# Paired node-number products, shorter but fewer ties of the gathers to VectorE, and logits copied once per group

## The chip, the cores and the metric

The kernel runs on one core of a Trainium2 chip. The metric is the device time of one execution in microseconds, the median of several runs. A profile of one execution stands beside it: the page, and answers drawn from its trace. In them PE is TensorE (PEld its weight loads), DVE is VectorE, ACT is ScalarE, POOL is GpSimd and SP is SyncE.

## The reference

Two graph layers over 6250 nodes of 256 features and 106250 edges, sorted by target, 6250 of them loops. Layer 0 sends each edge's source row through a small network of the edge's type, sums by target, applies gates and three more products, and normalizes. Layer 1 is attention with four heads:

```python
h = (x @ W).reshape(n, H, F)
e = leaky_relu(a_src[src] + a_dst[dst], 0.2)
ex = exp(e - m[dst])                       # m: the largest e of a target
alpha = ex / (denom[dst] + 1e-16)          # denom: the sum of ex of a target
out = segment_sum(h[src] * alpha[..., None], dst)
x = layernorm(x + relu(layernorm(out + bias + x)))
```

## The kernel before

**Tiles, windows, groups, pairs.** The 100000 edges that are no loops lie in 782 tiles of 128. Seven tiles (`WT`) are a window, two windows a group of up to 128 target nodes. A group's sum also takes the first tile of the next group, so it has 15 tile places (`GS`). In layer 1 two groups make a pair, the last four groups stand alone.

**Prologue, to 210 us.** Edges are sorted into place, the rows of layer 0's edge network are computed for all nodes and stored (`parts0`), and the first 60 gathers of layer 0 are made.

**Layer 0, about 210 to 1163 us.** A loop makes one pass per tile. In pass n GpSimd issues the gather of tile n (`gather`, L1717: 128 rows of 256 numbers by a list of indices, into one of ten buffers `G` of seven tiles), TensorE sums tile n - 4 into its group (`sum0`, L2175: a product with a one-hot matrix that VectorE made, L1832), and all chains that are under way take one step (`Steps`). Chains are written as generators; what they yield is the number of passes they rest. `turn` (L1924 to L1942) adds the loops and transposes a group's sums, `update` (L2006 to L2137) does the gates (first multiply of the gates L2019), products and the norm of up to four groups, stores layer 1's rows (`rows1`) and writes the attention numbers of the group's nodes as bfloat16 triples to `node3` (L2137).

**Layer 1, about 1163 us to the end.** The same kind of loop. Pass t gathers tile t (L1717 again, from `rows1`), the first 21 by `gather_early`. Four passes after its gather a window's logits are copied from its rows by ScalarE (L2626) to the pair's box `e`; the first tile of the next group follows (L2618). Then `weights` starts: a transpose on TensorE (L2378), scans over the edges on VectorE (L2385 to L2396), and the exponent (L2409). `weighted` (L2424 to L2430) multiplies gathered rows by them, `sum1` (L2546) sums by target, `finish` (L2444 to L2495) normalizes and stores.

**The node numbers.** Ahead of a pair, `ahead` loads the slot numbers of its edges (0 to 127 within the group, as bfloat16 in the dram list `slots`), the same list to all 128 partitions (`dB`, L2313). 12 passes later VectorE compares them with the partition's number (`ohT`, L2338: 15 x 128 columns), and TensorE multiplies each tile's one-hot matrix by the group's `node3` (L2345: 15 products of 24 columns), which gives the attention numbers of each edge's target; VectorE adds the triples (L2355). Targets are sorted, so the first seven tiles of a group (places 0 to 6) only hold slots below 64 and places 10 to 14 only slots from 64; `MID = (7, 10)` names these bounds, and the kernel takes another path where the chip finds that they don't hold.

**The order.** Everything is issued in the order in which the loop writes it down; each engine runs its own part of that order, and waits on semaphores hold up all that stands behind on the same engine. GpSimd's gathers are tied to VectorE by hand: `Pace.passes` notes at the end of each pass the last VectorE instruction written so far, and `hold` makes the gather of pass n wait for the one noted a distance of passes sooner:

```python
def hold(self, move, n, ahead):
    n -= self.first + ahead
    if n < 0:
        return
    tc.add_manual_dep(move.ins, self.passed[n].name, ...)
```

The distance is `AHEAD0` in layer 0 and `AHEAD1` plus a term in layer 1, which falls from 42 by one in six passes and rises by one in two over the last 42 passes.

Of the kernel before, what the change touches and what calls it, by code (L numbers as in the profile page):

```python
# [42 lines left out]
P = 128  # L43
N = 6250
D = 256
# [39 lines left out]
AHEAD_G = range(AHEAD_W // 2)  # L85
LATE = 3
CR = 16 * WT
AHEAD0 = 2 * WT
AHEAD1 = WT + 1
NOROW = NP + P // 2 - 1  # L90
SORTED = "the fast path runs only where the chip has found the edges sorted"

# [1547 lines left out]
def fast(  # L1640
# [46 lines left out]
    def at(ap, offset, dims):  # L1687
        return bass.AP(tensor=ap.tensor, offset=ap.offset + offset, ap=dims)
# [58 lines left out]
    class Pace:  # L1747
# [7 lines left out]
            self.passed.append(next(i for i in reversed(traced) if i.engine == ET.DVE))  # L1755

        def hold(self, move, n, ahead):
            n -= self.first + ahead
            if n < 0:
                return  # L1760
            tc.add_manual_dep(
                move.ins,
                self.passed[n].name,
                mybir.DependencyInfo(mybir.DependencyClass.Sync, mybir.DependencyReason.DATA),
                reason="rows come no sooner than they are wanted",
            )
# [489 lines left out]
    with (  # L2256
# [45 lines left out]
        def ahead(pair, box):  # L2302

            cut = ring(ep, [P, P + 1], F32, "cut", 3)
            of = ring(ep, [P, 2 * GS, 2 * H], F32, "of", 3)
            box.update(cut=cut, of=of)
            i0, n = pair[0] % 2, len(pair)
            if i0 == 0:
                box["dB"] = ring(ep, [P, 2, GS * P], BF16, "dB", 1)
            else:  # L2310
                box["dB"] = boxes[pair[0] - 1]["dB"]
            dB = box["dB"][:, i0 : i0 + n, :]
            nc.sync.dma_start(  # L2313
                dB.rearrange("p i e -> p (i e)"),
                at(slots, pair[0] * GS * P, [[0, P], [1, n * GS * P]]),
            )
            if pair in pairs[:2]:
                for i, g in enumerate(pair):
                    nc.sync.dma_start(
                        cut[i * GS * H : (i + 1) * GS * H, :],  # L2320
                        at(cuts, tiles_in(g)[0][0] * P, [[P, GS], [0, H], [1, P + 1]]),
                    )
            else:
                o = pair[0] % 2 * GS * H
                n = ((len(pair) - 1) * GS + len(tiles_in(pair[-1])[1])) * H
                pc = ring(tps, [P, P + 1], F32, "turn", 2)
                nc.tensor.matmul(
                    pc[:n, :],
                    pick[:, pair[0] % 8 // 2, o : o + n],
                    cut_all[:, pair[0] // 8, :],  # L2330
                    start=True,
                    stop=True,
                )
                nc.scalar.copy(cut[:n, :], pc[:n, :])
            yield 12 if len(pair) > 1 else 8
            for i, g in enumerate(pair):
                ohT = ring(ep, [P, GS, P], BF16, "ohT", 2)
                nc.vector.tensor_scalar(  # L2338
                    ohT.rearrange("p j e -> p (j e)"), dB[:, i, :], iota_p, None, op0=OP.is_equal
                )  # L2340
                yield 2
                n = len(tiles_in(g)[1])
                pn = ring(ops, [P, GS, 3, 2 * H], F32, "pn", 2)
                for j in range(n):
                    nc.tensor.matmul(  # L2345
                        pn[:, j, :, :].rearrange("p c a -> p (c a)"),
                        ohT[:, j, :],
                        node3[:, g, :, :].rearrange("p c a -> p (c a)"),
                        start=True,
                        stop=True,  # L2350
                    )
                    if j == WT:
                        yield 1
                yield 1
                nc.vector.tensor_reduce(  # L2355
                    of[:, i * GS : i * GS + n, :],
                    pn[:, :n, :, :].rearrange("p j c a -> p j a c"),
                    axis=AX.X,
                    op=OP.add,
                )  # L2360
                yield 1
# [56 lines left out]
        def weighted(g, w, o, n, of, ex, top):  # L2418

            if g not in ohs:  # L2420
                ohs[g] = ring(ep, [P, (2 * WT - 2) * LOW + 3 * P], F32, "oh1", 2)
                one_hot(ohs[g], g, slot, MID[1])
            gw = ring(ep, [P, WT if n > 1 else 1, D + 2 * H], F32, f"gw{min(n, 2)}", 4)[:, :n, :]
            nc.vector.tensor_mul(  # L2424
                gw[:, :, HA:],
                top[:, o : o + n, :],
                first[:, WT * w : WT * w + n, None].to_broadcast([P, n, H]),
            )
            nc.scalar.copy(gw[:, :, D:HA], ex[:, o : o + n, :])  # L2429
            nc.vector.tensor_mul(  # L2430
                gw[:, :, :D].rearrange("p j (h f) -> p j h f", h=H),
                of[:, :n, :D].rearrange("p j (h f) -> p j h f", h=H),
                ex[:, o : o + n, :, None].to_broadcast([P, n, H, F]),
            )
            return gw

        def finish(g, ps):
# [73 lines left out]
        pair_of = {g: p for p in pairs for g in p}  # L2511
        boxes = {p[0]: {} for p in pairs}
        sums, queue, read, ohs, k3s, left, written = {}, [], set(), {}, {}, {}, []
        results = {}

        def sum1():

            while late and len(queue) < 8:
                piece = late.pop(0)
                g, w, o, n = piece[:4]  # L2520
                gw = weighted(*piece)
                queue.extend((g, WT * w + j, gw[:, j, :]) for j in range(n))
            if not queue:
                return
            g, t, gw = queue[0]
            if g not in sums and g >= 2 and g - 2 not in read:
                return
            queue.pop(0)
            if g not in sums:
                sums[g] = ring(eps, [P, D + 2 * H], F32, "fps1", 2)  # L2530
                left[g] = len(tiles_in(g)[1])
                u = everyone
                if g % 2 == 0:
                    k3s[g // 2] = ring(fp, [P, 2, 3, D], F32, "k3", 2)
                of = k3s[g // 2].rearrange("p i c f -> p i (c f)")
                if len(pair_of[g]) == 1:
                    nc.sync.dma_start(of[:, g % 2, :], kept[g // 2, :, g % 2, :])
                elif g % 2 == 0:
                    nc.sync.dma_start(of, kept[g // 2])
            begins = left[g] == len(tiles_in(g)[1])  # L2540
            left[g] -= 1
            j = t - 2 * WT * g
            to, cols = place(j, MID[1])
            ohj = ohs[g][:, cols]
            ends = left[g] == 0 or j in (WT - 1, TC - 1 - 2 * WT * g)
            nc.tensor.matmul(sums[g][to, :], ohj, gw, start=begins, stop=ends)  # L2546
            if left[g] == 0:
                run.start(finish(g, sums[g]), 1)

        def aheads():  # L2550
            for pair in pairs:
# [42 lines left out]
        while t < TC + LAG or late or queue or run.chains:  # L2594
            if EARLY <= t < TC:
                w = t // WT
                if t % WT == 0:
                    G[w] = ring(rowsp, [P, WT * HA], F32, "G", 10).rearrange(
                        "p (j f) -> p j f", f=HA
                    )  # L2600
                move = gather(G[w][:, t - WT * w, :], rows1, idx1[:, t : t + 1])
                pace.hold(move, t, AHEAD1 + max(0, 6 * WT - (t - EARLY) // 6, 3 * WT - (TC - t) // 2))
            k = t - LAG
            if 0 <= k < TC:
                if k < EARLY:
                    complete(k)
                w = k // WT
                g = w // 2
                pair = pair_of[g]
                box = boxes[pair[0]]  # L2610
                if k % (2 * WT) == 0:
                    if g == pair[0]:
                        box["e"] = ring(ep, [P, 2 * GS, H], F32, "e", 3)
                    if g:

                        old = pair_of[g - 1]
                        ob = boxes[old[0]]
                        nc.scalar.copy(  # L2618
                            ob["e"][:, old.index(g - 1) * GS + 2 * WT, :], G[w][:, 0, D:HA]
                        )  # L2620
                        if old is not pair:
                            run.start(weights(old, ob))
                if k == tiles_of(w)[0][-1]:
                    o = pair.index(g) * GS + WT * (w % 2)
                    own = len(tiles_of(w)[0])
                    nc.scalar.copy(box["e"][:, o : o + own, :], G[w][:, :own, D:HA])  # L2626
                    if w == NW - 1:
                        run.start(weights(pair, box))
            sum1()
# [67 lines left out]
```

## Time and profile before

| | |
|---|---|
| median of 9 runs | 2180.26 us (2178.31 to 2184.77) |
| the profiled execution | 2181.07 us, of which the span of its instructions 2179.3 us |
| busy over the span | PE 1586.9 us (73%), DVE 1320.1 (61%), ACT 498.8 (23%), POOL 1543.9 (71%) |
| gathers of layer 0, L1717 | 722, mean 958 ns, first 210.4, last 1130.1 us |
| gathers of layer 1, L1717 | 21 + 761, mean 956 and 961 ns, 1131.3 to 2126.6 us |
| weighted rows on VectorE, L2430 | 167, 248.9 us |
| slot comparisons on VectorE, L2338 | 56 of 128x1920, 42.1 us |
| node-number products, L2345 | 837, 41.0 us on PE |
| logit copies on ScalarE, L2626 | 112, mean 212 ns; idle 190.2 us before them, 149.8 of it for gathers |
| DMA over the span | 346.12 MB, 159 GB/s |

A row of the page's groups names the line, the engine, the operation, what is written and read with shapes and the count; behind the bar come busy time and the mean of one, then the engine's idle time just before, and what ended most of it. "issue" is time in which the engine waited for nothing that the profile shows. A row of the timeline gives start and length in us, and in brackets the idle time before it. Idle time of an engine that is not the bottleneck costs nothing, and a busy share hides the short gaps between instructions.

### The profile page before, as it was taken

The numbers are of one execution on the slowest core, as the hardware profiler recorded it, in microseconds if no ns is written. First come the engines' busy times: TensorE is split into PE (matmuls) and PEld (weight loads), VectorE is DVE, ScalarE is ACT, GpSimd is POOL, SyncE is SP. The second block draws the span as 40 slices with busy tenths as digits, with TensorE's granted clock in tenths as the row PEclk, the third lists the DMA queues.
The fourth block names the chain that finished last, engine by engine and source line by source line (L and its number), as shares of the span: only waits on it lengthen the run. The fifth ranks groups of instructions, "written<-read, shape, count | busy, mean of one in ns | idle before, by whom it ended". The sixth has DMA issues, their size and how long they took to land.

```text
span 2179.3 us, 23269 instructions
## 1 busy us (share of the span) xinstructions
PE 1586.9 (73%) x6390; PEld 850.3 (39%) x6390; DVE 1320.1 (61%) x3622; ACT 498.8 (23%) x1538; POOL 1543.9 (71%) x1610
## 2 busy tenths in 40 slices
PE   8988998788888888888986656465565555555564
PEld 5656543333433333333554333233232333333332
DVE  8854354434243433434443788888887777878786
ACT  3333132122211222122341121221211211121112
POOL 2466677777777777777777777777777777777770
PEclk9999999999899998999997777777776767677776
DMA  5355645445554555445555555555555555555551
GB/s 158 114 173 173 187 148 184 146 139 172 167 153 136 164 167 168 139 147 173 184 156 174 167 175 156 174 167 157 179 163 160 163 160 166 157 171 151 172 153 37
DMA packets 146105, 346.12 MB, mean 159 GB/s; under 512 B 36154, under 2 KB 66720, under 8 KB 145965
## 3 DMA queue, kind: packets, MB, share of 16 engines
q0 software_dynamic: 76048, 207.99, 34.0%
q1 hardware_dynamic: 67741, 133.51, 17.5%
q10 hardware_dynamic: 2176, 3.05, 0.4%
q8 instruction: 52, 0.85, 0.2%
q14 instruction: 88, 0.72, 0.1%
HBM read 291.90 MB, written 52.52 MB: 158 GB/s over the span
## 4 chain that ended last, share of the span: by engine, by line
PE 31%; DVE 21%; DMA 17%; issue 11%; POOL 8%; ACT 4%; DVEq 0%; POOLq 0%; ACTq 0%
PE fps L2175 11%; DMA G<-parts,fidx 9%; POOL G L1717 8%; DMA G<-rows,fidx 7%; PE fpg L2006 6%; DVE gw L2430 5%; PE fps L2546 4%; DVE oh L1832 3%; PE fpg L2092 2%; PE fps L2288 1%; PE fpm L1571 1%; DVE fst L2476 1%; PE fpg L2054 1%; ACT fy L2484 1%; DVE ohT L2338 1%
## 5 line engine op out<-in xcount | busy, mean ns | idle before, releaser
L1717 POOL DMA_INDIRECT G<-rows,fidx x761 | 731.1, 961 | 233.3 <-issue 132.9
L1717 POOL DMA_INDIRECT G<-parts,fidx x722 | 692.0, 958 | 230.7 <-issue 156.3
L2546 PE MATMUL fps<-gw,oh 128*64 128x264 f32 (+1 forms) x1674 | 469.5, 471 | 187.7 <-DVE gw L2430 187.7
L2175 PE MATMUL fps<-G,oh 128*64 128x257 f32 (+1 forms) x1674 | 498.2, 417 | 116.2 <-DMA G<-parts,fidx 99.0
L2546 PEld LDWEIGHTS fps<-gw,oh 128*64 128x64 f32 (+1 forms) x1674 | 241.4, 177 | 335.1 <-DVE gw L2430 202.2
L2175 PEld LDWEIGHTS fps<-G,oh 128*64 128x64 f32 (+1 forms) x1674 | 210.0, 156 | 378.4 <-DMA G<-parts,fidx 175.0
L2430 DVE TENSOR_TENSOR gw<-G,bank 128x1792 f32<-128x1792 f32 (+1 forms) x167 | 248.9, 1491 | 57.3 <-ACT gw L2429 56.0
L2006 PE MATMUL fpg<-faT,fWihT 128*128 128x512 f32 (+2 forms) x432 | 172.8, 525 | 0.2 <-DVE faT L1942 0.2
L1832 DVE TENSOR_TENSOR oh<-bank,fslot 128x448 f32<-128x448 f32 (+2 forms) x318 | 156.5, 547 | 8.9 <-ACT bank L2409 6.1
L1924 DVE TENSOR_SCALAR kind<-fps 128x1 f32<-128x1 f32 x112 | 12.4, 152 | 207.9 <-PE fps L2175 207.9
L1571 PE MATMUL fpm<-fWrT,fhT 128*128 128x256 f32 x392 | 94.9, 393 | 13.6 <-DVE fms L1579 13.3
L2126 DVE COPY nd<-hr 128x4 f32<-128x4 f32 x53 | 9.9, 188 | 152.3 <-ACT hr L2098 152.3
L2006 PEld LDWEIGHTS fpg<-faT,fWihT 128*128 128x128 f32 x432 | 73.2, 196 | 68.4 <-issue 56.5
L1557 PE MATMUL fph<-fxc,fWrT 128*128 128x512 f32 (+1 forms) x208 | 89.9, 582 | 5.1 <-DMA fWrT<-in_WrT_dram 4.6
L1605 POOL DMA_INDIRECT G<-parts,fidx x60 | 62.0, 1033 | 42.4 <-DVE fms L1579 19.0
L2345 PE MATMUL pn<-node,ohT 128*128 128x24 bf16 x837 | 41.0, 180 | 68.2 <-DVE ohT L2338 61.6
L1571 PEld LDWEIGHTS fpm<-fWrT,fhT 128*128 128x128 f32 x392 | 75.1, 196 | 33.2 <-DVE fms L1579 12.6
L2478 ACT ACTIVATE frs<-fmv,eps_c 128x1 f32<-128x1 f32 x112 | 32.9, 294 | 237.0 <-DVE gw L2424 153.6
L2484 ACT ACTIVATE fy<-fy,frs 128x256 f32<-128x256 f32 x112 | 66.9, 597 | 87.3 <-DVE frs L2481 87.0
L2378 PE MATMUL turn<-fident,e 128*120 128x128 f32 (+2 forms) x30 | 12.0, 399 | 96.2 <-ACT e L2618 96.2
L2345 PEld LDWEIGHTS <-ohT 128*128 128x128 bf16 x837 | 34.2, 103 | 109.5 <-DVE ohT L2338 76.0
L2092 PE MATMUL fpg<-Wx,fyT 128*128 128x264 f32 x224 | 72.5, 451 | 3.0 <-ACT fyT L2083 3.0
(348 smaller groups left out, 1967.9 us busy)
## 6 DMA issues: line engine op xcount, KB each, us to landing
dB<-slots SPq DMA_DIRECT2D x26, 960.0 KB
kept<-keep SPq DMA_DIRECT2D x26, 768.0 KB
k<-kept SPq DMA_DIRECT2D x26, 768.0 KB
loop<-parts SPq DMA_DIRECT2D x55, 256.0 KB
parts<-fms SPq DMA_DIRECT2D x49, 256.0 KB
G<-parts,fidx POOLq DMA_INDIRECT x782
G<-rows,fidx POOLq DMA_INDIRECT x761
out_dram<-fy SPq DMA_DIRECT2D x56, 128.0 KB
```

The source lines that it names most:

```text
L1557: nc.tensor.matmul(ph[:, :cols], WrT_s[:, r, k, m * P : (m + 1) * P], xc[:, k, :cols], start=(k == 0), stop=(k == 1),)
L1571: made = nc.tensor.matmul(pm[:, r, :], hT[:, r, k, j * P : (j + 1) * P], WrT_s[:, r, k, :], start=(k == 0), stop=(k == 1),)
L1605: nc.gpsimd.indirect_dma_start(out=of[:, n % WT, :D], out_offset=None, in_=parts0[: 2 * P * block, :], in_offset=bass.IndirectOffsetOnAxis ...
L1717: return nc.gpsimd.indirect_dma_start(out=to_tile, out_offset=None, in_=table, in_offset=bass.IndirectOffsetOnAxis(ap=idx, axis=0),)
L1832: nc.vector.tensor_tensor(to[:, o : o + len(js) * n].rearrange("p (j s) -> p j s", s=n), iota_s[:, None, cols].to_broadcast([P, len(js), n ...
L2006: nc.tensor.matmul(pg[:, :cols], WihT_s[:, k, c * P : (c + 1) * P], aT[:, k, :cols], start=(k == 0), stop=(k == 1),)
L2092: nc.tensor.matmul(ph[u, :], hs[i][:, k, u], Wx[:, k, :], start=(k == 0), stop=(k == 1))
L2175: nc.tensor.matmul(sums[g][to, :], ohj, got[t], start=begins, stop=ends)
L2345: nc.tensor.matmul(pn[:, j, :, :].rearrange("p c a -> p (c a)"), ohT[:, j, :], node3[:, g, :, :].rearrange("p c a -> p (c a)"), start=True ...
L2430: nc.vector.tensor_mul(gw[:, :, :D].rearrange("p j (h f) -> p j h f", h=H), of[:, :n, :D].rearrange("p j (h f) -> p j h f", h=H), ex[:, o ...
L2484: nc.scalar.activation(y, y, AF.Identity, bias=m, scale=r)
L2546: nc.tensor.matmul(sums[g][to, :], ohj, gw, start=begins, stop=ends)
```

## The change

Four edits. **Ties:** `AHEAD0` goes from 14 to 6 and `AHEAD1` from 8 to 4, and only gathers whose number divides by four are tied. **Products:** `dB` and `ohT` have 10 tile places in place of 15. The lower 64 partitions hold the slots of places 0 to 9; the upper 64 hold those of 10 to 14 in the first five places and their own 7 to 9; the rest of the upper half keeps the -1 of a memset. One product of the first five places serves two tiles, j and j + 10, against `node2`, whose lower rows have the node numbers in the first 24 columns and whose upper rows have them in the last 24; ScalarE fills its two blocks by two copies a group, of four buffers in turn. The list is loaded by three transfers. **Logits:** both windows of a group are copied when its second is there, the second first. **Weighted rows:** the multiply at L2430 no longer waits for the gathers of its rows, since the weights come from logits copied out of the same rows.

```diff
-AHEAD0 = 2 * WT
-AHEAD1 = WT + 1
+AHEAD0 = WT - 1
+AHEAD1 = WT - 3
+EVERY = 4
...
         def hold(self, move, n, ahead):
+            if n % EVERY:
+                return
...
-                box["dB"] = ring(ep, [P, 2, GS * P], BF16, "dB", 1)
+                box["dB"] = ring(ep, [P, 2, MID[1] * P], BF16, "dB", 1)
...
-            nc.sync.dma_start(
-                dB.rearrange("p i e -> p (i e)"),
-                at(slots, pair[0] * GS * P, [[0, P], [1, n * GS * P]]),
-            )
+            for ps, c0, j0, jn in (
+                (low_s, 0, 0, MID[1]),
+                (high_s, 0, MID[1], GS - MID[1]),
+                (high_s, MID[0], MID[0], MID[1] - MID[0]),
+            ):
+                nc.sync.dma_start(
+                    dB[ps, :, c0 * P : (c0 + jn) * P],
+                    at(slots, (pair[0] * GS + j0) * P, [[0, LOW], [GS * P, n], [1, jn * P]]),
+                )
...
             for i, g in enumerate(pair):
-                ohT = ring(ep, [P, GS, P], BF16, "ohT", 2)
+                halves = node2[g % 4]
+                for h, ps in enumerate((low_s, high_s)):
+                    nc.scalar.copy(
+                        halves[ps, h, :], node3[ps, g, :, :].rearrange("p c a -> p (c a)")
+                    )
+                ohT = ring(ep, [P, MID[1], P], BF16, "ohT", 2)
...
-                for j in range(n):
-                    nc.tensor.matmul(
-                        pn[:, j, :, :].rearrange("p c a -> p (c a)"),
-                        ohT[:, j, :],
-                        node3[:, g, :, :].rearrange("p c a -> p (c a)"),
-                        start=True,
-                        stop=True,
-                    )
-                    if j == WT:
+                po = pn.rearrange("p j c a -> p j (c a)")
+                for j in range(MID[1]):
+                    if j < GS - MID[1]:
+                        to, of_n = po[:, j : MID[1] + j + 1 : MID[1], :], halves
+                    elif j < MID[0]:
+                        to, of_n = po[:, j, :], halves[:, 0, :]
+                    else:
+                        to, of_n = po[:, j, :], node3[:, g, :, :].rearrange("p c a -> p (c a)")
+                    nc.tensor.matmul(to, ohT[:, j, :], of_n, start=True, stop=True)
+                    if j == MID[1] // 2:
                         yield 1
...
-            nc.vector.tensor_mul(
+            made = nc.vector.tensor_mul(
                 gw[:, :, :D].rearrange("p j (h f) -> p j h f", h=H),
...
+            for move in brought.get(w, [])[:n]:
+                tc.declare_no_dep(
+                    made.ins, move.ins, reason="the weights come from logits of these rows"
+                )
...
+        node2 = [ep.tile([P, 2, 6 * H], BF16, name=f"node2_{i}") for i in range(4)]
+        for halves in node2:
+            nc.vector.memset(halves, 0.0)
+        nc.vector.memset(ring(ep, [P, 2, MID[1] * P], BF16, "dB", 1), -1.0)
...
                 move = gather(G[w][:, t - WT * w, :], rows1, idx1[:, t : t + 1])
+                brought.setdefault(w, []).append(move)
...
-                if k == tiles_of(w)[0][-1]:
-                    o = pair.index(g) * GS + WT * (w % 2)
-                    own = len(tiles_of(w)[0])
-                    nc.scalar.copy(box["e"][:, o : o + own, :], G[w][:, :own, D:HA])
+                if k == tiles_of(w)[0][-1] and (w % 2 or w == NW - 1):
+                    for v in (w, w - 1) if w % 2 else (w,):
+                        o = pair.index(g) * GS + WT * (v % 2)
+                        own = len(tiles_of(v)[0])
+                        nc.scalar.copy(box["e"][:, o : o + own, :], G[v][:, :own, D:HA])
```

More of the change, by code (lines that the diff above doesn't have):

```diff
@@ L2513, in fast @@
         sums, queue, read, ohs, k3s, left, written = {}, [], set(), {}, {}, {}, []
-        results = {}
+        results, brought = {}, {}
         def sum1():
```

## The prediction

> **What bounds the kernel now.** I read the page first (costliest groups, slices), then the time by stages, the waits of GpSimd, and last the timeline of the places that these point to.
>
> ```profile
> L1717 POOL DMA_INDIRECT G<-rows,fidx x761 | 731.1, 961 | 233.3 <-issue 132.9
> L1717 POOL DMA_INDIRECT G<-parts,fidx x722 | 692.0, 958 | 230.7 <-issue 156.3
> ```
>
> ```profile
> 400.00:600.00 200.00, 170.82 (x528) 75.11 (x528) 74.24 (x260) 42.33 (x106) 151.78 (x159) 0.91 0.52 158
> ...
> 1500.00:1700.00 200.00, 113.19 (x579) 64.96 (x576) 162.77 (x399) 40.14 (x167) 151.84 (x159) 0.73 0.55 164
> ```
>
> The stages list PE, PEld, DVE, ACT and POOL, busy time and (count). TensorE leads in layer 0 and VectorE in layer 1, yet GpSimd issues 159 gathers in 200 us in both, one in 1.258 us. Its waits say that little holds it up:
>
> ```profile
> POOL G L1717 <- issue: 293.3, 963, 0.3
> ```
>
> 963 gaps, none over 0.3 us. A gather costs 0.95 + 0.30 = 1.25 us, so 76% busy is a full engine; starts of neighbouring gathers lie 1.25 us apart (median) whether the gather carries one, two or three waits. From 210 to 2127 us the kernel is a train of 722 + 21 + 761 = 1504 gathers, 1880 us of 1917. What moves the end is a stall of the train, a stretched gather, or the 53 us behind it.
>
> **Shorter ties, layer 0.** With a distance of 14 passes no tie bound here: the VectorE instruction waited for had ended 1.7 us or more before its gather. With 6 they bind at the start, where TensorE works off the sums gathered ahead and VectorE waits for it. Gathers are numbered from 60 (210.45 us), and number 96 starts at 262.04. After the change it waits for the last VectorE instruction of pass 90, by the built kernel's order the first multiply at L2019:
>
> ```profile
> 262.04 0.95 POOL L1717 DMA_INDIRECT G<-parts,fidx  x1 [0.30 <-issue]
> ```
>
> ```profile
> 269.06 0.68 DVE L2019 TENSOR_TENSOR fgg<-fgg,fgi 128x512 f32<-128x512 f32 x1
> ```
>
> It ends at 269.74. The one tie that did bind before (below) let its gather start 0.27 us after the end, so number 96 starts at 270.0, 8.0 us late. Numbers 84, 88 and 92 are late by 0.2, 2.1 and 6.1 us in the same way, which is contained in the 8.0; 104 needs 276.60 and would start at 280 anyway. All later gathers queue behind. TensorE does not notice at once:
>
> ```profile
> 250.00:270.00 20.00, 20.00 (x77) 10.50 (x76) 8.36 (x22) 3.34 (x4) 15.13 (x17) 1.00 0.56 159
> ```
>
> ```profile
> 336.95 0.65 PE L2175 MATMUL fps<-G,oh 128*64 128x257 f32 x2 [0.58 <-DMA G<-parts,fidx]
> ```
>
> It is full, and waits for a gather for the first time at 336.95. But from there to 1108 it waits for gathers again and again (99 us in all), and the train has no slack to catch up in. So a delay passes to the end of layer 0 whole, and on into layer 1, which starts from it: **+8.0 us**. Bounds: 0, if something later absorbs it, and 8.0 plus the 1.3 us of the next tie that comes close (gather at 313.5), if VectorE moves with the train.
>
> **Shorter ties, layer 1.** VectorE starts this layer behind. Measured from a gather's start to the end of its pass's last VectorE instruction it is 38 us behind at 1163, 22 at 1200, 10 at 1411, 4.5 at 1482 (medians over 28 passes, with swings of some 5 us), and from 1590 to 2050 never over 3.1. The distance falls by one pass in six gathers until about 1480, then is 8 before and 4 after. Before, it bound once:
>
> ```profile
> 1487.92 0.95 POOL L1717 DMA_INDIRECT G<-rows,fidx  x1 [0.30 <-issue]
> 1490.58 0.94 POOL L1717 DMA_INDIRECT G<-rows,fidx  x1 [1.71 <-DVE frs L2481]
> ```
>
> 2.66 instead of 1.25 us: 1.4 lost. With 4 passes less, the gather at 1485.42 waits for that same L2481 (end 1490.31, plus 0.27): 5.2 us. Against it stands that VectorE is faster by then: one-hot comparisons (L2338) take 0.715 us for 1920 columns; 1280 take between two thirds of that and no less, I take 0.22 us saved. 18 groups pass from 1163 to 1485, 18 x 0.22 = 4.0. Loss 1.2 against 1.4 before: **-0.2**. Bounds -1.4 (no tie binds) and +3.8 (VectorE gains nothing). Later, the smallest slack of a tied gather is 3.2 us, so the steady part is untouched.
>
> Fewer ties by themselves (waits on VectorE at gathers 878 to 358 in the built order) bring nothing: the 1.25 us do not depend on the number of waits.
>
> **The comparison beside the train.** The one stretched gather that repeats in layer 1 lies beside L2338:
>
> ```profile
> 1606.43 0.95 POOL L1717 DMA_INDIRECT G<-rows,fidx  x1 [0.30 <-issue]
> 1607.68 1.24 POOL L1717 DMA_INDIRECT G<-rows,fidx  x1 [0.31 <-DMA G<-rows,fidx]
> ```
>
> ```profile
> 1607.39 0.71 DVE L2338 TENSOR_SCALAR ohT<-dB,fiota_p 128x1920 bf16<-128x1920 bf16 x1
> ```
>
> Over all 56 the gathers beside L2338 exceed 0.947 us by 6.6 us together. A third less comparison takes a third of it: **-2.2 us**, bounds 0 and -6.6.
> The Trainium skill (SBUF — State Buffer, Who interferes with whom) says that such an instruction and GpSimd share a port pair as an exclusive lock, and that the later one fully blocks. By that the gather would lose the 0.42 us that L2338 still had to run, the trace shows 0.29; if every L2338 blocked for all its 0.715 us, 40 us would be lost now and 13 won, and the whole sum would be near -6. I go by the rows.
>
> **Products.** 837 products and loads become 560, 280 of them twice as wide. TensorE does eight in 0.39 us and only 2.0 us of VectorE's waits (reduction at L2355) are for them: 0, cover gone 2.0 won. The added ScalarE copies of node numbers, 112 of 0.208 us (row of L2137), are 23 us on an engine busy 23%, issued two passes (2.5 us) ahead of the products: 0; without that cover 0.4 us a group, 23 us over layer 1 if TensorE and then VectorE waited each time. Five memsets at the start of layer 1 (the widest 2560 columns; L1787 wrote 672 in 0.62, so 2.4) fall where VectorE sits idle 6.8 us until 1168.78 for its first list (L2274): 0, and 3 if that list came at once.
>
> **The slot lists.** 30 transfers of up to 960 KB become 90 of 64 partitions, 61% of the bytes. SyncE takes 0.32 us for an issue (L2313), 19 us more, and between issues it is idle for 10 us and more (1602.66 to 1624.96). Queued behind are the loads of kept rows and the output; VectorE never waited for a list (idle before L2338: 0.0), and a list is asked for 12 passes, 15 us, ahead: 0; bounds -1 and, if all three were late by an issue each, 26 x 0.64 = 17.
> The Trainium skill (DMA: Bandwidth & Descriptors, Rules for kernel authors) speaks against this edit: transfers to disjoint partition halves serialize, one of 128 partitions is to be used. With its fit of 2.0 us plus bytes over 436 GB/s, three in a row would take some 7.4 us for a pair, one 4.3 (estimates from that page); 3 us more under a cover of 15 leave the sum as it is.
>
> **Logits.** The 112 copies of 0.212 us stay; both of a group now stand behind its last gather, so ScalarE no longer stops in mid-group, and the transpose comes one copy later: 0.2 us once per pair, in layer 1's steady part inside the train's slack of 3.2 us: 0; bounds -1 and +1 at the end. The 493 waits for gathers dropped at the weighted rows (L2430) are hidden too: of 57.3 us idle before them 56.0 are ScalarE's copy, so 1.3 at most.
>
> **Behind the last gather** (2126.6 to 2179.3) VectorE and TensorE work alone, and VectorE is already 3.5 to 4.7 us behind from 2086. Five comparisons fall there: 5 x 0.22 = **-1.1**, bounds +1 and -2.
>
> **Sum.** +8.0 - 0.2 - 2.2 - 1.1 = +4.5 us. The profiled execution (2181.07 us, span 2179.3) becomes 2185.6; it lies 0.8 over the median of 2180.26, so I predict 2184.8 us.
>
> **Rivals.** (1) *The delay in layer 0 is absorbed.* TensorE is full until 336 us and again near 1000 to 1135 (122 of 130 us), and if it, not the train, sets the end of layer 0, the 8.0 costs nothing: 2180.3 - 0.2 - 2.2 - 1.1 = 2176.8, no change. With the whole 6.6 of stretched gathers won it is 2172.4, faster; the point from which it decides is 3.1 us won at the stretched gathers with layer 0 at zero. For it: 20.00 of 20 us. Against it: the waits for gathers after 336, up to 1108. 0.2 for both, 0.08 of it past the point.
> (2) *Layer 1's ties bind in full*, because VectorE's 0.22 us are lost in waits for ScalarE (idle before L2430): +3.8 for -0.2, 2188.8. Against it: VectorE is 83% busy there. 0.2.
> (3) *The comparisons hold the train for their full length*: a third of 56 x 0.715 us is 13.3 us won for 2.2, 2173.7, faster; it decides from 11.1 us won on. Against it: all stretched gathers of layer 1 together exceed by 10.4 us. 0.05.
> (4) *Three list transfers or the added copies come late* and the products with them: 17 us, 2201.8. For it: nothing but the number of issues. 0.05.
> My forecast has the remaining 0.5, from 2181 to 2188.
>
> **Numbers.** A measurement of this kernel tells 0.2% (4.4 us) from no change: faster is below 2175.9, slower above 2184.6. Faster: 0.08 of (1), 0.05 of (3) and 0.01 of the forecast: 0.14. Slower: 0.19 of (2), 0.05 of (4), and 0.27 of the forecast's 0.5, whose middle lies just above the bound: 0.51. Same: the rest, 0.35. The range reaches from (1) at 2176 to (2) with the second tie of layer 0 (1.3): 2190.
>
> **What would show it.** Right: GpSimd with one wait of some 7 to 8 us for VectorE near 262 us, gathers 1.25 us apart whatever they wait for, layer 1's first gather some 8 us later than 1163.5, no wait or one of 1 to 3 us near 1490, L2338's comparison at 0.5 us and its stretched gather at 0.2 over. Wrong: no long wait in layer 0; or layer 1 starting at 1163 in spite of it; or waits of GpSimd spread over the steady part.

## The result, and the profile after

The changed kernel takes 2192.49 us (median of 10 runs, 2189.47 to 2199.04); the kernel before, run beside it, 2181.63 (32 runs). The ratio is 1.0053, 95% interval 1.0045 to 1.0061: slower by 11 us, where 4.5 were forecast and 2190 was the upper end of the range. The profiled execution took 2190.16 us, its span is 2188.3, 9.0 more than the span before.

The page's rows of GpSimd's gathers, then a row of GpSimd's waits (us in total, times, longest):

```profile
L1718 POOL DMA_INDIRECT G<-rows,fidx x761 | 734.4, 965 | 232.7 <-issue 187.9
L1718 POOL DMA_INDIRECT G<-parts,fidx x722 | 691.6, 958 | 239.3 <-issue 178.5
```

```profile
POOL G L1718 <- issue: 370.0, 1204, 3.7
```

The longest gap put down to "issue" was 0.3 us, now it is 3.7; layer 1's gathers take 965 ns on average instead of 961, which over 761 of them is 3.3 us; layer 0's have kept their 958. So there are two places to look at: a stall in layer 0 and a stretch in layer 1. The steady middle of both layers (us; then busy time and count of PE, PEld, DVE, ACT, POOL; the granted clock of TensorE as a share of full speed, the DMA share, GB/s) is what it was, 159 to 160 gathers in 200 us. The traces have the clock at full or at half speed only, so 0.70 is a mean:

```profile
400.00:600.00 200.00, 162.73 (x531) 70.95 (x530) 74.81 (x264) 42.22 (x105) 151.57 (x160) 0.97 0.52 159
1500.00:1700.00 200.00, 108.77 (x483) 61.65 (x483) 155.37 (x394) 42.63 (x190) 151.87 (x159) 0.70 0.56 153
```

The timeline of GpSimd at the head of layer 0, rows of late gathers (0.30 is the usual gap):

```profile
249.10 0.94 POOL L1718 DMA_INDIRECT G<-parts,fidx  x1 [0.76 <-DVE faT L1945]
...
257.49 0.95 POOL L1718 DMA_INDIRECT G<-parts,fidx  x1 [3.70 <-issue]
...
265.00 0.95 POOL L1718 DMA_INDIRECT G<-parts,fidx  x1 [2.80 <-DVE faT L1945]
...
271.63 0.95 POOL L1718 DMA_INDIRECT G<-parts,fidx  x1 [1.93 <-DVE fgg L2022]
```

These are four tied gathers, four apart. Each idle time less 0.30 is the stall: 0.46 + 3.40 + 2.50 + 1.63 = 8.0 us. "issue" at 257.49 is the same wait with its releaser not found. The gather that was at 262.04 is at 271.63.

In layer 1 VectorE and GpSimd, side by side:

```profile
1734.78 0.42 DVE L2508 SCALAR_TENSOR_TENSOR fy<-fy,k 128x256 f32<-128x256 f32 x1
1735.12 0.54 DVE L2351 TENSOR_SCALAR ohT<-dB,fiota_p 128x1280 bf16<-128x1280 bf16 x1
1735.23 1.25 POOL L1718 DMA_INDIRECT G<-rows,fidx  x1 [0.30 <-DVE fy L2508]
```

The comparison is shorter as forecast (0.54 us for 0.71), and the gather that starts beside it still takes 1.25 us, 0.30 more than its neighbours. It is not the only such instruction. Line 2508 (L2490 before) runs into gathers where no comparison follows, too:

```profile
1714.70 0.42 DVE L2508 SCALAR_TENSOR_TENSOR fy<-fy,k 128x256 f32<-128x256 f32 x1
...
1714.88 1.07 POOL L1718 DMA_INDIRECT G<-rows,fidx  x1 [0.30 <-issue]
```

In the trace of before 5 gathers of layer 1 start beside it in this way and lose 0.6 us together, in that of the changed kernel 20, which lose 2.4.

The trace cut at the first and last gather of each layer gives the whole account. All times are us, and the runs below the first two rows are told of in the next section:

| kernel | first gather | layer 0's train | between | layer 1's train | end | span |
|---|---|---|---|---|---|---|
| before | 210.45 | 919.64 | 33.37 | 963.13 | 52.70 | 2179.29 |
| changed | 211.62 | 927.69 | 33.30 | 965.77 | 49.89 | 2188.27 |
| changed, again | 210.44 | 927.78 | 33.01 | 965.04 | 49.53 | 2185.80 |
| all ties back | 213.26 | 921.58 | 33.73 | 966.06 | 50.37 | 2185.00 |
| layer 0's ties back | 212.01 | 920.64 | 33.34 | 966.94 | 49.29 | 2182.22 |
| layer 0's distance back | 212.44 | 921.10 | 33.68 | 966.66 | 49.93 | 2183.81 |
| changed, beside that | 212.70 | 933.82 | 31.93 | 967.99 | 49.89 | 2196.33 |
| all ties back, comparison later | 211.58 | 922.93 | 33.11 | 958.79 | 50.12 | 2176.53 |

Between the first two rows: +1.2 ahead of the trains, +8.05 in layer 0, -0.1 between, +2.6 in layer 1, -2.8 at the end, together +9.0. The 1.2 lie in the prologue, which the change does not touch, and the second profile of the changed kernel has them not.

### The profile page after: what moved, and what is told of

Its sections match the earlier page's. It is cut to its first block, busy times and chain, and to the rows that moved or that the text cites. A ratio compares the mean times of both kernels' runs of the same rounds, so it can differ in the third digit from the quotient of the medians.

```text
span 2188.3 us, 21961 instructions
## 1 busy us (share of the span) xinstructions
PE 1574.4 (72%) x6113; PEld 839.3 (38%) x6113; DVE 1310.7 (60%) x3627; ACT 512.5 (23%) x1650; POOL 1547.0 (71%) x1610
## 4 chain that ended last, share of the span: by engine, by line
PE 29%; DVE 28%; DMA 14%; issue 9%; POOL 9%; ACT 5%; SPq 0%; ACTq 0%; DVEq 0%; POOLq 0%
PE fps L2178 9%; DMA G<-parts,fidx 9%; POOL G L1718 9%; DVE gw L2444 8%; PE fpg L2009 6%; PE fps L2564 5%; DVE oh L1835 4%; DMA G<-rows,fidx 3%; DVE fst L2494 1%; PE fpg L2095 1%; DVE ohT L2351 1%; PE fpm L1572 1%; PE fps L2291 1%; ACT fy L2502 1%; DVE fy L2479 1%
## 5 line engine op out<-in xcount | busy, mean ns | idle before, releaser
L2178 PE MATMUL fps<-G,oh 128*64 128x257 f32 (+1 forms) x1674 | 493.2, 410 | 133.2 <-DMA G<-parts,fidx 116.2
L2365 PE MATMUL pn<-node,ohT 128*128 128x24 bf16 (+1 forms) x560 | 35.6, 192 | 69.6 <-DVE ohT L2351 65.9
L2365 PEld LDWEIGHTS <-ohT 128*128 128x128 bf16 x560 | 28.5, 107 | 111.2 <-DVE ohT L2351 77.1
```

The source lines that it names most:

```text
L2178: nc.tensor.matmul(sums[g][to, :], ohj, got[t], start=begins, stop=ends)
L2365: nc.tensor.matmul(to, ohT[:, j, :], of_n, start=True, stop=True)
```

## The experiments

**The ties and the products apart, first sitting** (a sitting is a set of runs made together on one chip). Four kernels. The first puts layer 0's ties back:

```diff
-AHEAD0 = WT - 1
+AHEAD0 = 2 * WT
...
-            if n % EVERY:
+            if not self.first and n % EVERY:
```

> Theory A (the changed kernel's extra time is 8.0 us of stalls of the gather train in layer 0, and some 3 us in layer 1 that are not its ties): with layer 0 tied as before, layer 0 from its first to its last gather takes 919.6 us again instead of 927.7, and the time is 8.0 us below the changed kernel, 2 to 3 us above the kernel before. Rival B (the delay of layer 0 would have been absorbed, and something else costs the time): within 3 us of the changed kernel. Rival C (the products and lists cost what is left): as A in layer 0, so this run alone does not tell C from A.

The second puts all ties back (also `AHEAD1 = WT + 1`, and no `EVERY`):

> All ties as before; products, logits and the dropped wait as in the changed kernel. Theory A: layer 1's ties cost less than 1 us, so this is within 1.5 us of the run with layer 0's ties back; against the kernel before 1 to 3 us slower, with some 9 us of stretched gathers beside the slot comparison where the kernel before has 6.6. The prediction's own terms (2.2 us won beside the comparison, 1.1 won at the end): 3.3 us faster than before. Rival D (layer 1's ties cost the 3.8 us of the prediction's bound): 3 us or more below the run with layer 0's ties back.

The third is the kernel before with the new ties and nothing else:

> The kernel before with the ties alone. Theory A: 8.0 us in layer 0, and in layer 1 the 3.8 us that the prediction put on the ties if VectorE gains nothing (no shorter comparison here to make up for them): 11.8 us slower than before. If layer 1's ties do not bind even so: 8.0 less the 1.4 us of the one bound tie, 6.6 us slower. Rival B: within 2 us of before.

The fourth is the kernel before with the paired products and their lists and nothing else:

> The kernel before with the paired products and three list transfers alone. Prediction's terms: 3.3 us faster (2.2 beside the comparison, 1.1 at the end). Theory A (what a comparison costs the train goes by where it falls in a gather, not by its length): between 1 us faster and 3 us slower, with a comparison of 0.55 us instead of 0.72. Rival C (lists and copies come late): VectorE or TensorE waits for dB or for node copies, 3 us slower or more.

None of these theories was about the regime that these four ran in. There the kernel before took 2738.01 us (26 runs), and TensorE was granted a clock of 0.76 on average instead of 0.84. The first three ratios in the order above: 0.9923 (0.9894 to 0.9952), 0.9974 (0.9948 to 1.0), 0.9905 (0.9873 to 0.9937); products alone 0.9973 (0.9952 to 0.9994). The page of the kernel with layer 0's ties back has this chain and these slices of the clock:

```profile
PE 33%; DVE 26%; another core or an unknown queue 22%; issue 11%; ACT 4%; DMA 2%; POOL 1%; ACTq 0%; SPq 0%; DVEq 0%; POOLq 0%
...
PEclk9977988788877878879866676676766767676766
```

GpSimd is 1% of the chain there. The "unknown queue" is stretches in which TensorE begins next to nothing while VectorE and ScalarE stand still, such as the second row here, from the windows of the same kernel:

```profile
640.00:656.00 16.00, 13.09 (x55) 6.45 (x54) 8.78 (x26) 2.46 (x6) 12.04 (x14) 1.00 0.39 117
656.00:673.00 17.00, 0.34 (x2) 0.10 (x2) 0.00 (x0) 0.00 (x0) 10.03 (x11) 0.61 0.31 92
```

TensorE is busy for 0.34 us of these 17, while GpSimd goes on with 11 gathers until they too wait for VectorE. The clock was at half for 1299 us of this execution, for 701 us of that of the kernel before at 2181. But the standing still is nearly all of the longer time: this same kernel ran later at a clock of 0.84 (below), with a span of 2182.2 us instead of 2700.5, 518 less. Stretches of over 4 us in which TensorE, VectorE and ScalarE all stand still make 475 us here (55 of them, up to 16.9), and 4.8 us there (one). What they wait for the trace does not show. With the train no longer the bound, what is won or lost at the train says nothing on the forecast, and the new ties even help, 0.9905 on their own. Why they do was not settled.

**The changed kernel again.**

> The changed kernel itself, unaltered. Where the granted clock is 0.84 to 0.85 and the kernel before takes some 2181 us, every theory expects the 2192 us already seen. Where the granted clock is 0.76 and the kernel before takes some 2738 us, the theory that a full train of gathers pays for every stall expects it slower there too, by about the same 11 us; the theory that TensorE, held to half its clock for half the time, is the bound there, and that the train has slack, expects the sum of what its parts did there: layer 1's ties -16 us, layer 0's -7 us, the rest -5 us, so some 2710 us, a ratio of 0.990.

Measured at a clock of 0.84: 2190.69 us, the kernel before 2181.46, ratio 1.0048 (1.0031 to 1.0064). The result repeats, and the layer-0 train repeats to 0.1 us.

**Four once more, and the clock at 0.76 again.** The kernel before took 2765.86 us in this sitting. Layer 0's ties back:

> The changed kernel with layer 0's ties put back to a distance of 14 and onto every gather; layer 1 keeps the new ties. Measured before this run: 2181 us for the kernel before, 2191 to 2192 for the changed one. Theory 1 (four stalls of GpSimd at the head of layer 0, 8.0 us, come straight off the end): 2183 to 2184. Rival (layer 0's stalls are taken up by slack between the layers, and the loss sits in layer 1): 2190 to 2192.

0.9894 (0.9867 to 0.9921). All ties back:

> The changed kernel with all ties as before: only the paired products, their lists, the logits' copies and the dropped wait are left of the change. Theory 1 (what layer 1 lost comes with the paired products, whose shorter comparisons now fall on a gather each): the layer-1 train still 2.5 us longer than before, the end 2 to 3 us shorter, so 2181 to 2184, and within 1 us of the run with layer 1's ties kept. Rival (layer 1's shorter and fewer ties cost it): 3 us or more below that run, at 2178 to 2181.

2747.25 us, 0.9934 (0.9913 to 0.9954). Products alone:

> The kernel before with the paired products and their lists alone; ties, logits and waits as before. If the products bring the stretch of layer 1's gathers, the layer-1 train is 2 to 3 us longer here as well and the time is that of the run with all ties back, within 1 us. If the logits' copies or the dropped wait bring it, the train is as before (963 us) and the time 2 to 3 us lower.

2746.14 us, 0.9939 (0.9913 to 0.9965). All ties back, with the comparison made twice instead of 56 times:

```diff
+                ohT = ohT_made.get(g % 2)
+                if ohT is None:
+                    ohT = ohT_made[g % 2] = ring(ep, [P, MID[1], P], BF16, "ohT", 2)
...
```

> All ties back, and the comparison of line 2351 made for two groups only and reused for the other 54, so its output is not the reference's. Theory 1 (a gather that starts beside a comparison is lengthened by it, and the train is the bound): the excess of layer 1's gathers over 0.946 us falls by the 9 us that stood beside comparisons, to some 4 or 5 us, and the time by 8 to 10 us below the run with all ties back. Rival (another VectorE instruction moves into its place and stretches the gather as much): less than 3 us below. Second rival (VectorE's 31 us of comparisons delay the sums and so the end): more than 12 us below.

2729.85 us, 0.9878 (0.9854 to 0.9903): 17 us below the run with all ties back, where theory 1 had 8 to 10 and the second rival more than 12. The excess of layer 1's gathers over 0.946 us is 1.3 us in its trace and 6.3 in that with all ties back, so shorter gathers make 5 us of the 17 at most. The forecasts in us fail here as in the first sitting. Two things carry over: with and without the logits' copies and the dropped wait the kernel takes the same time in both sittings (2747.25 and 2746.14; 2733.04 and 2730.36), so these edits do nothing that can be measured there; and the regime belongs to the sitting and not to the chip, since the chip of these four ran the next experiment at 2187 us for the kernel before.

**All ties back, at a clock of 0.84.**

> All ties as before; the paired products, their lists, the logits' copies and the dropped wait stay. Where the granted clock is 0.84 and the kernel before takes 2181 us: theory 1 (ties cost 8.0 us in layer 0 and nothing in layer 1; the paired products' comparisons lengthen layer 1's gathers by some 3 us and the end gives 2 to 3 back) 2181 to 2184, a layer-0 train of 920 us, a layer-1 train of 965 to 966 us; rival (layer 1's shorter and fewer ties lengthen its train) 2178 to 2181 and a layer-1 train of 963 us or less. Where the clock is 0.76: 0.993 to 0.997 of the kernel before, as in the two runs there.

2185.94 us beside 2187.17, ratio 0.9995 (0.9984 to 1.0006). So what the change makes slower is in the ties; the rest of it together does nothing that the interval shows. Its trains say how: 966.06 us in layer 1, as long as with the new ties. Layer 1's 2.6 us are not from the ties, which the rival said. They come with the rest, and the end gives them back. Products, logits and the dropped wait were not taken apart at this clock, so which of them moves layer 1 and the end is not shown.

**The comparison, 0.2 us later.** In the trace with all ties back I set the start of each comparison against the start of the last gather before it, and the two gathers around it against the usual 0.946 us. The loss is a matter of when the comparison starts. From 0.95 to 1.15 us the next gather is longer by what the comparison still has to run beside it, less 0.12 to 0.14 us, in 38 cases of 38; from 0.5 to 0.94 next to nothing; from 0.08 to 0.25 at most 0.05; the two at 0.41 and 0.46 lengthen the gather that is running, by 0.13 and 0.17. In the kernel before, 17 comparisons start at 1.17 to 1.22 us, that is 0.03 to 0.08 us ahead of the next gather, and lengthen nothing. The changed kernel has none there and 24 at 1.05 to 1.15, the dearest place. A rule of the Trainium skill (SBUF — State Buffer, Who interferes with whom) is an exclusive lock in which the later one waits in full; the gather that starts second does lose here, but 0.13 us less than the overlap, and from 1.17 us on nothing, although the comparison still starts first. To test it, one instruction that does nothing useful goes ahead of each comparison:

```diff
+                nc.vector.tensor_add(lull, iota_f, iota_f)
                 ohT = ring(ep, [P, MID[1], P], BF16, "ohT", 2)
...
+        lull = ep.tile([P, P], F32, name="lull")
```

> All ties as before, products and logits as changed, and one more VectorE instruction (a sum of two 128x128 f32 tiles, some 0.19 us) ahead of each of the 56 comparisons of line 2351, so that each starts 0.19 us later. In the profile with all ties back, 23 comparisons start 1.07 to 1.13 us after the start of the last gather and lengthen the next one by 0.23 to 0.29 us, 15 start at 0.95 to 1.01 us and lengthen it by 0.12 to 0.18 us, and those that start at 0.02 to 0.23 us lengthen nothing. Theory P (where in the gather's 1.25 us the comparison falls decides, not how long it is): the 23 move to 0.01 to 0.07 us of the next gather and cost nothing, the 15 to 1.14 to 1.20 us and cost 0.3 us each or nothing, so the excess of layer 1's gathers beside comparisons falls from 8.5 us to between 1 and 6 us and the time by 3 to 8 us, although VectorE has 10 us more to do. Rival (each comparison beside the train costs by its length alone, whenever it comes): the excess stays at 8 to 9 us and the time within 1 us. Second rival (VectorE's extra 10 us reach the end): 2 to 10 us slower.

2177.42 us beside 2183.75: 0.9971 (0.9962 to 0.998). More work, and faster than both kernels; against all ties back (0.9995) it is 5.2 us by the ratios, which were measured in two sittings. The same place in the two timelines, first with all ties back, then with the instruction added:

```profile
1802.12 0.43 DVE L2506 SCALAR_TENSOR_TENSOR fy<-fy,k 128x256 f32<-128x256 f32 x1
1802.46 0.55 DVE L2349 TENSOR_SCALAR ohT<-dB,fiota_p 128x1280 bf16<-128x1280 bf16 x1
...
1802.61 1.22 POOL L1718 DMA_INDIRECT G<-rows,fidx  x1 [0.30 <-DVE fy L2506]
```

```profile
1797.17 0.42 DVE L2507 SCALAR_TENSOR_TENSOR fy<-fy,k 128x256 f32<-128x256 f32 x1
1797.51 0.28 DVE L2348 TENSOR_TENSOR lull<-fiota 128x128 f32<-128x128 f32 x1
1797.71 0.55 DVE L2350 TENSOR_SCALAR ohT<-dB,fiota_p 128x1280 bf16<-128x1280 bf16 x1
...
1797.67 0.95 POOL L1718 DMA_INDIRECT G<-rows,fidx  x1 [0.30 <-DVE fy L2507]
```

The comparison is as long as it was. It starts 0.15 us ahead of a gather above, 0.04 us behind one below, and the gather takes 0.95 us for 1.22. The starts say the same: the next gather follows 1.52 us later above (1804.13) and 1.25 us later below (1798.92). Over layer 1:

```profile
L1718 POOL DMA_INDIRECT G<-rows,fidx x761 | 735.3, 966 | 232.0 <-issue 126.5 <-DVE gw L2436 14.9 <-DVE sm L2462 11.3
```

```profile
L1718 POOL DMA_INDIRECT G<-rows,fidx x761 | 727.3, 956 | 232.8 <-issue 111.2 <-DVE gw L2437 15.2 <-DVE frs L2498 11.8
```

8.0 us less of gather time, and a train of 958.79 for 966.06. By the place of the comparison (us after the last gather's start; number of comparisons, and what the gathers around them lost in us):

| | 0 to 0.35 | to 0.48 | to 0.94 | to 1.05 | to 1.165 | later | sum |
|---|---|---|---|---|---|---|---|
| before | 8: 0.3 | 1: 0.3 | 17: 1.9 | 13: 4.2 | 0 | 17: 0 | 6.7 |
| changed | 4: 0 | 2: 0.3 | 12: 0.1 | 14: 2.0 | 24: 6.7 | 0 | 9.1 |
| all ties back | 4: 0.1 | 2: 0.3 | 12: 0 | 15: 2.2 | 23: 6.0 | 0 | 8.6 |
| comparison later | 19: 0.3 | 1: 0.1 | 19: 0.1 | 4: 0.7 | 7: 2.2 | 6: 0 | 3.4 |

Theory P holds on the place, within its 1 to 6 us of excess and 3 to 8 us of time; both rivals fall. How sharp the place is shows in the last row: the 6 that start at 1.16 us cost 0.33 us each, the 6 from 1.18 us nothing. Its words "not how long it is" go too far: at 0.95 to 1.05 us a comparison of 0.71 us costs 0.32 us (13 of them, before), one of 0.55 us 0.14 (14, changed). At a given start the shorter one does cost less; the starts moved.

The comparison is 5.2 of the 8.0 us. Line 2508 follows the same rule (L2506 with all ties back, L2507 here): it takes 0.42 us, and 21 of them start 1.04 to 1.07 us after a gather's start with all ties back and cost 2.2 us together. In the run with the instruction added 3 do, for 0.3 us, and 14 start at 0.43 to 0.45 and cost nothing, as 18 do before at 0.44 to 0.46. So the delay moved more than the comparison, and helped at both.

**Layer 0's ties back, at a clock of 0.84.**

> The changed kernel with layer 0's ties put back to a distance of 14 and onto every gather; layer 1 keeps the new ties. The changed kernel took 1.0048 and 1.0053 of the kernel before, and with all ties back 0.9995. Where the granted clock is 0.84: theory 1 (the four stalls at the head of layer 0 are the whole cost of the ties, 8.0 us or 0.0037) a layer-0 train of 920 to 922 us, a layer-1 train of 965 to 966 us, and 0.999 to 1.001; rival (the ties cost in layer 1 too, the 3 to 4 us by which 1.0053 over 0.9995 exceeds 8.0 us) 1.001 to 1.003.

2184.7 us beside 2184.91: 0.9997 (0.9988 to 1.0006). Layer 0's ties are the whole of the loss; layer 1's new ties cost nothing that the times show, 0.9997 against 0.9995 with them back. In its profile two of them do bind, for 2.3 us together, where with all ties back none does, and its layer-1 train is 966.94 us, 0.9 longer and just over the 965 to 966 of theory 1.

**Distance or number of ties, on one chip.** By those ratios layer 0's ties cost 11 to 12 us, and the stalls in the profile are 8.0. One kernel has the changed line `AHEAD0 = 2 * WT` and nothing else undone, the other is the changed kernel.

> The changed kernel with layer 0's distance alone put back to 14 passes; still only every fourth gather is tied, in both layers. Theory 1 (the distance of 6 makes GpSimd wait for VectorE at the head of layer 0; how many gathers are tied brings and costs nothing): a layer-0 train of 918 to 922 us and 8 to 12 us less than the changed kernel beside it, 0.999 to 1.001 of the kernel before. Rival (part of the 10 to 12 us by which the changed kernel's time stood above the run with layer 0's ties back, more than the 8.0 us of stalls in its profile, comes from tying only every fourth gather): 2 to 4 us above 1.000.

> The changed kernel, unaltered, on the same chip as the run with layer 0's distance back, so that the cost of that distance is read from times of one sitting and from two profiles of it. If the stalls at the head of layer 0 are all: the layer-0 train 8 us longer than in that run and the medians 8 us apart. If the distance costs elsewhere too: the medians 10 to 12 us apart, and the trains or the stretch before the first gather show where.

With the distance back: 2184.76 us, 1.0011 (1.0002 to 1.002). The changed kernel beside it: 2193.71 us, 1.0046 (1.0033 to 1.006). The distance of 6 costs 8.95 us by the medians, between the two forecasts of 8 and of 10 to 12. The changed kernel's profile, of the longest of its five executions (2198.12 us), has the four stalls of 8.0 us and others later, the largest of 2.87 us:

```profile
1030.25 0.69 DVE L2022 TENSOR_TENSOR fgg<-fgg,fgi 128x512 f32<-128x512 f32 x1 [5.39 <-ACT fgg L2017]
...
1031.21 0.94 POOL L1718 DMA_INDIRECT G<-parts,fidx  x1 [3.17 <-DVE fgg L2022]
```

The tied gather starts 0.27 us after L2022 ends, as at the head of the layer. The stretch of time just before, in this execution and in that of the kernel with the distance back:

```profile
1005.00:1020.00 15.00, 12.97 (x35) 6.34 (x34) 5.05 (x29) 4.21 (x11) 11.35 (x13) 0.76 0.75 229
```

```profile
1005.00:1020.00 15.00, 15.00 (x42) 5.63 (x40) 3.81 (x10) 6.22 (x11) 11.34 (x13) 1.00 0.59 189
```

The clock was 0.76 in one and 1.00 in the other. That a slower TensorE made VectorE late enough for the tie to bind is what these rows suggest; it is one execution, and was not forced. What they show is that the distance of 6 leaves room for such stalls in the middle of the layer, of which the other two profiles of the changed kernel have some 0.1 us at most. Those two are of executions 2.3 and 3.0 us under their medians, this one 4.4 over. The 11 to 12 us against 8 can thus be in part stalls that come in some executions; the rest is within the ratios' own uncertainty of some 2 us. Whether the number of ties counts for anything stays open. 1.0011 lies just outside theory 1's range and at the lower end of the rival's 2 to 4 us; the layer-0 train, 921.10 us, is theory 1's. With every gather of layer 0 tied it was 0.9997, on another chip, and the two intervals overlap.

## Why the prediction failed, step by step

**Layer 0's ties, +8.0: right in the profile, short in some executions.** Same gathers, same instructions of VectorE, 8.05 us in the profile, and 8.0 us at layer 1's first gather once the prologue's 1.2 are taken off: the 33 us between the layers did not shrink. Nothing absorbed it (rival 1). I had named one wait of 7 to 8 us near 262; it was spread over four waits, which the same paragraph had counted as contained in the 8.0. The upper bound of 9.3 was too low: one execution lost 12.7 (933.82 against 921.10), 1.6 of it in longer gathers. I had looked for ties that nearly bind in one trace alone.

**Layer 1's ties, -0.2: within the bounds.** The one wait before was 1.4 us, the one after is 1.15 - 0.30 = 0.85:

```profile
1496.60 0.95 POOL L1718 DMA_INDIRECT G<-rows,fidx  x1 [1.15 <-DVE frs L2499]
```

This moves from execution to execution: with the new ties in layer 1 the waits are 0.8 us in the second profile of the changed kernel, 2.3 and 2.2 in the two runs with layer 0 put back, 3.4 in the changed kernel beside the latter. Against the 1.4 of before that is -0.6 to +2.0 us. Rival 2's 3.8 us did not come, and undoing the ties there moved nothing in the times. The 0.22 us that each comparison was to save were 0.17 (0.546 for 0.715, medians).

**The comparison beside the train, -2.2: this step failed.** The loss beside it was to fall by 2.2 us; it rose from 6.7 to 9.1 us, and with other stretched gathers layer 1's excess went from 11.2 to 14.5. The words "a third less comparison takes a third of it" treat the loss as a share of the comparison's length. The dear part is the overlap with a gather that has yet to start, so it is set by the comparison's length and above all by where it starts in a cycle of 1.25 us; the step had no term for the start. The change moved 24 of them to the dearest place and took 17 from the one where they cost nothing. The sum also had the other stretched gathers at no change; beside L2508 they went from 0.6 to 2.4 us, for the same reason. Why the starts moved was not taken apart; it was not the ties, since they lie there with all ties back as well. The trace of before had it all: 17 comparisons at 1.17 to 1.22 us with no stretched gather were in it, and I looked only at the sum. My bounds, 0 and -6.6, excluded a loss for no reason that I had given. Rival 3, a lock for the comparison's full length, had the same fault from the other side.

**Behind the last gather, -1.1:** -2.8. The bound was -2. At the measured 0.17 us the five comparisons are 0.9; what the other 1.9 are was not looked into. All runs with products, logits and the dropped wait at this clock have an end of 49.3 to 50.4 us, so it repeats.

**Products, lists, logits, dropped wait, 0: right in sum.** With all ties back the ratio is 0.9995, which is layer 1's loss and the end's gain together. An issue of a list took 0.60 us (median) where 0.32 was reckoned, and the lists have 60% of the bytes, not 61; of the 90 transfers VectorE waited for one, for 5.7 us at the start of layer 1, ahead of a layer that begins with a backlog. (The Trainium skill's rule in DMA: Bandwidth & Descriptors, Rules for kernel authors, spoke against three transfers for one; going against it cost nothing that shows here. The same page gives the fit that the prediction used for transfers issued by GpSimd; these are SyncE's, and no run here has their duration.)

**The sum.** 8.05 - 0.1 + 2.6 - 2.8 + 1.2 = 9.0 in the profile against +4.5: 4.5 us more. Layer 1's train is 5.0 us off (+2.6 for -2.4), which is the comparison's step and its like: 2.4 more beside the comparison, 1.9 beside L2508, about 1 less at other gathers and 0.6 less at the tie. The prologue's variation adds 1.2, and the end gave 1.7 back. The medians say 11 rather than 9; the profiled execution took 2190.16 us, 2.3 under the median. By the times the miss lies elsewhere in part: with all ties back 0.9995 is 1.1 us won where the terms without the ties say 3.3, so 2.2 us are missing there, with an uncertainty as large; and the ties, 1.0046 to 1.0053 with them against 0.9995 to 1.0011 with layer 0's or all back, cost 7.6 to 12.7 us for the 7.8 of the sum.

## What to carry to other kernels

When one engine issues a full train, a delay at its head reaches the end in whole, and a tie that is tight in one trace can bind more often in others. When two engines get in each other's way, do not scale the loss with an instruction's length alone: plot it against the time at which the instruction starts within the train's cycle, before and after, and ask where the change moves that start. Look at every instruction that shares the cycle, not only the one that was changed. Here a delay of 0.2 us won 5 us, where a third less of the comparison, with the rest of the edits but the ties, had won nothing that shows.

## What the runs showed of the hardware that was not expected

- An added VectorE instruction, which delays each comparison by 0.2 us, made the kernel faster: 0.9971 of before (interval 0.9962 to 0.998) with it, 0.9995 (0.9984 to 1.0006) without it.
- A comparison of 0.55 us that starts 0.95 to 1.15 us into a gather's cycle lengthens the next gather by the overlap less 0.13 us; the f32 instruction of line 2508, 0.42 us at 1.05 to 1.09 us, does the same. A comparison that starts at 0.49 us runs 0.77 us itself, to the next gather's start, and lengthens nothing: there it is VectorE that loses.
- In two sittings the kernel before took 2738 and 2766 us instead of 2181 to 2187, at a granted clock of 0.76; one of the two chips ran it at 2187 in another sitting. Of the 518 us between two profiles of one kernel, 470 were stretches of over 4 us in which TensorE, VectorE and ScalarE all stood still, and ties that cost 0.5% at a clock of 0.84 gained there.
- GpSimd's gathers keep 1.25 us from start to start whatever number of waits they carry: the changed kernel's profile has the same 159 to 160 of them in 200 us with a quarter of the ties.
